# Two-layer graph network on one core: a fourth chunk of the second pass by gathered lists, and dense tiles for the first 128 nodes in five blocks

## The chip, the core and the metric

The kernel runs on one core of one Trainium2 chip. Time is device time in microseconds (us), the median of three runs. A core has TensorE (PE in the profile; PEld are its weight loads), VectorE (DVE), ScalarE (ACT), GpSimd (POOL), and SyncE (SP), which here only issues transfers. ACT and POOL issue transfers as well. All arithmetic on PE is float32 but for the small matmuls that make lists; a float32 matmul appears in the trace as two instructions.

## The reference

There are 3327 nodes with 512 features, and a sparse adjacency matrix `adj` (0.27% of it nonzero, more in the rows and columns of the first nodes, and the whole diagonal).

```python
h = jnp.maximum(_layernorm(x), 0.0)                     # layer 0
x = x + adj @ (relu(adj @ (h @ W1) + b1) @ W2) + b2     # 512 -> 128 -> 512
h = jnp.maximum(_layernorm(x), 0.0)                     # layer 1
attn_a = sigmoid(concat([adj @ h, h]) @ Wa.T + ba)
attn_b = sigmoid(concat([adj @ h, h]) @ Wb.T + bb)
hh = h @ W_sa
e = where(adj != 0, exp(-leaky_relu(s_left[:, None] + s_right[None, :], 0.01)), 0)
x_a = (e / (sum(e) + 1e-5)) @ hh
x_b = adj @ (h @ W_gcnb) + b_gcnb
out = x + sigmoid(attn_a * x_a + attn_b * x_b)
```

`s_left` and `s_right` are two products of `hh` with halves of `a_sa`.

## The kernel before

The rows are padded to 3328, 26 blocks of 128 nodes; the transposed adjacency `adjT` is in HBM. The kernel goes over the graph three times.

**First pass** (the loop around line 660): u = h W1 for all blocks, then for each chunk of columns the sum over all 26 row blocks j, acc_u += u[j]^T adjT[j, chunk], each from a dense load of adjT (512 KB a load, six buffers). The chunks, in the order `back`, are blocks 22-25, 18-21, 14-17, 10-13, 2-5, 6-9 and 0-1. The result, after relu, is g (128 features a node), kept on chip and also stored as `g_dram`.

While a chunk passes, VectorE reduces it to a flag for each node and each group of 32 columns: does the node have an edge into the group (line 670)? In the next chunk's time `make_lists` turns the flags into lists of node numbers, with scans, small matmuls (p_list, line 573) and comparisons. A list of block i has `rooms[i]` places of 64 nodes for each of its four groups; block 0 (the "hub") has none and stays dense. Some of the nodes are left out of the lists because a dense tile takes them: `extra[i]` counts such tiles, one for the block's own diagonal (`OWN`) and one for the first 64 nodes (`TOP`). These tiles are loaded in the first pass by `load_own` (line 210 on) over ACT's queue, two DMAs of 16 KB each. If a list were too short, a flag is raised, and a guarded part at the kernel's end does the work again densely.

With the lists, POOL gathers from HBM with indirect DMAs (line 181), one for each place and half: the column pieces of adjT (128 pieces of 32 numbers, `ae`, by `gather_adj`), rows of g (`g_row`, 128 rows of 512 bytes) and rows of the second layer (`hr`, `rows`: 128 rows of 2080 bytes). Column pieces are gathered one at a time behind chosen matmuls (`gather_behind`) in the first pass, and later where `gather_one` and `fetch_ae` have room.

**Second pass**: adj times g. The last `LISTED = 3` chunks (12 blocks) are done by lists in `list_sums` (matmul at line 911): for each of a block's rooms + extra pairs k, four small matmuls (64 nodes x 32 columns) of the gathered columns with the gathered rows of g, with the block's own g, or with `g_top`, the g of the first 64 nodes. Then ACT copies the sums (line 921), PE turns them (pt_s, line 926), ACT copies again (line 931). The other chunks, 3.5 of 512 columns, are done densely in `dense_sums` (line 957), with adjT loaded again. Then for each block `make_row` adds the layer's result to x (px, line 752; line 756), normalizes, makes the scores, and stores the row to `h_dram`.

What PE does in this pass is written out by hand in `PLAN`, a letter and a count each: d one dense matmul of `dense_sums`, s the sums of one listed block, t the turn of a listed chunk, x a row (`make_row`), l the turning of scores, h one hub matmul (block 0 of the third pass needs all rows: `add_hubs`, line 804, with acc_hub from `a_hub` and from the exponentials e_hub), e the making of such an exponential on DVE and ACT. PE takes the steps in this order. `MADE` gives the order in which dense (d) and listed (l) chunks' rows are made. Each step has a planner's cost (`STEP`, 0.93 for d, x and h, 1.1 for s, 0.6 for t, 0.5 for l). Whenever `SPACE` = 1.4 of them have passed since the last and more than `QUIET` = 20 are left, `gather_one` issues a gather behind the PE's last matmul: the next g row where one of the 24 row buffers is free, else the next column piece. Hub matmuls that the plan leaves over are done after it, in `rest_of_hubs`.

**The passage**: SP then issues the loads of W_gcnb, of the weights for the logits, of `h_top` (the rows of the first 64 nodes), of `w_left`, and of the first blocks' own rows (`h_own`, line 1087). h_top, a scratch `junk` and w_left lie in the space of `a_hub`, which the hub's matmuls and exponentials must have left.

**Third pass**: attention, block by block from 25 down to 1, with block 0 first from the hub's sums. For each pair k of a block, `attend` makes the exponentials and `sums` (line 1171) does four 64x64 matmuls over 512 features for each of two accumulators; `turn` (line 1185), `weigh` (p_b line 1225, p_a line 1233) and `finish` give the output. Blocks are pipelined: PE does p_b and p_a of one block, the turn of the next and the sums of the one after. For each block `fetch_ae(2)` gathers two more column pieces, and a block that still lacks pieces gathers them before its rows. A block's row gathers are held back (`pace`) until the sums of three or four blocks earlier are done.

Block i's number of pairs k is rooms[i] + extra[i]. Before: 4 for blocks 14, 15, 17, 18, 21 and 24; 3 for 16, 19, 20, 22, 23 and 25; 5 for 10 and 11; 4 for 12 and 13; 5 for 7 and 8.

## Time and profile before

| what | us |
|---|---|
| median of three runs | 720.23 |
| lowest, highest | 717.16, 721.58 |
| the profiled execution's own time | 803.64 |
| its span, first to last instruction | 801.8 |
| first pass in the span | 0 to 237.8 |
| plan of the second pass | 237.8 to about 404 |
| passage (rest of the hub, first loads and gathers) | about 404 to 450 |
| third pass | about 450 to 802 |

The profile is of one execution, and it is longer than the runs without a profile. In a row of a timeline stand the start and the length in us, the engine, the line of the kernel, the operation, output<-inputs, and how many instructions were merged; what stands in brackets is how long the engine was idle before it, and what released it ("issue": nothing that the profile names; "remote": a releaser that it can't name). A group's mean is in ns. POOL made 424 gathers: 178 of columns, 68 of g rows, 178 of second-layer rows. Of the column gathers 98 were issued before 237.8 us, 39 after 404.

### The profile page before, as it was taken

The numbers are of one execution on the slowest core, as the hardware profiler recorded it, in microseconds if no ns is written. First come the engines' busy times: TensorE is split into PE (matmuls) and PEld (weight loads), VectorE is DVE, ScalarE is ACT, GpSimd is POOL, SyncE is SP. The second block draws the span as 40 slices with busy tenths as digits, with TensorE's granted clock in tenths as the row PEclk, the third lists the DMA queues.
The fourth block names the chain that finished last, engine by engine and source line by source line (L and its number), as shares of the span: only waits on it lengthen the run. The fifth ranks groups of instructions, "written<-read, shape, count | busy, mean of one in ns | idle before, by whom it ended". The sixth has DMA issues, their size and how long they took to land.

```text
span 801.8 us, 11934 instructions
## 1 busy us (share of the span) xinstructions
PE 727.4 (91%) x3723; PEld 392.0 (49%) x3723; DVE 486.1 (61%) x1532; ACT 204.7 (26%) x494; POOL 456.8 (57%) x487
## 2 busy tenths in 40 slices
PE   8999949988999799797996589899999999999995
PEld 7775424433554344344543255344555445555554
DVE  6878947988963245455573077347567466575642
ACT  6770000000000234444460123022223122131311
POOL 2400556766765667766727646776766766676400
PEclk9999969999979999998998699899999999999998
DMA  8789949988849999983368456756665766877410
GB/s 273 250 299 310 304 135 292 322 276 266 274 127 337 337 320 332 365 263 125 119 223 281 128 157 208 224 160 179 213 190 179 224 197 201 241 229 226 135 52 31
DMA packets 105882, 180.47 MB, mean 225 GB/s; under 512 B 21361, under 2 KB 38161, under 8 KB 105810
## 3 DMA queue, kind: packets, MB, share of 16 engines
q1 hardware_dynamic: 63776, 111.91, 41.3%
q0 software_dynamic: 22112, 54.46, 23.9%
q10 hardware_dynamic: 19922, 13.25, 5.3%
q8 instruction: 31, 0.51, 0.3%
q14 instruction: 41, 0.34, 0.1%
HBM read 157.64 MB, written 22.26 MB: 224 GB/s over the span
## 4 chain that ended last, share of the span: by engine, by line
PE 83%; issue 7%; DVE 3%; DMA 2%; another core or an unknown queue 2%; ACT 1%; ACTq 0%; SPq 0%; DVEq 0%
PE acc_u L660 19%; PE acc L1171 14%; PE p_b L1225 12%; PE p_a L1233 12%; PE acc_g L957 9%; PE acc_hub L804 3%; PE pu L381 3%; PE px L752 3%; PE ptt L1185 3%; DMA a<-in_adjT_dram 1%; PE pt L373 1%; PE p_list L573 1%; PE acc_s L911 1%; PE pl L1103 1%
## 5 line engine op out<-in xcount | busy, mean ns | idle before, releaser
L181 POOL DMA_INDIRECT ae<-in_adjT_dram,row_a x178 | 185.3, 1041 | 137.9 <-DVE jb L584 57.4
L660 PE MATMUL acc_u<-a,rows 128*128 128x512 f32 (+1 forms) x364 | 166.7, 596 | 3.9 <-issue 2.9
L181 POOL DMA_INDIRECT hr<-h_rows,row_h x114 | 120.3, 1055 | 54.0 <-issue 27.4
L670 DVE TENSOR_REDUCE most<-a 128x32 f32<-128x1024 f32 (+1 forms) x104 | 104.2, 1010 | 12.9 <-DMA a<-in_adjT_dram 9.9
L1225 PE MATMUL p_b<-W_g_sb,tyT 128*128 128x257 f32 x416 | 101.8, 395 | 8.9 <-issue 7.1
L1233 PE MATMUL p_a<-W_sa_sb,tyT 128*128 128x512 f32 (+3 forms) x224 | 97.0, 576 | 3.4 <-DVE f L1047 1.9
L660 PEld LDWEIGHTS acc_u<-a,rows 128*128 128x128 f32 x364 | 68.6, 200 | 63.7 <-issue 59.3
L181 POOL DMA_INDIRECT rows<-h_rows,row_h x64 | 67.9, 1061 | 54.6 <-PE acc L1171 22.6
L1225 PEld LDWEIGHTS p_b<-W_g_sb,tyT 128*128 128x128 f32 x416 | 78.3, 194 | 42.2 <-issue 16.0
L181 POOL DMA_INDIRECT g_row<-g_rows,row_h x68 | 70.9, 1042 | 34.5 <-issue 14.9
L957 PE MATMUL acc_g<-a,g 128*128 128x512 f32 (+1 forms) x208 | 86.4, 555 | 1.0 <-DMA a<-in_adjT_dram 0.7
L1200 DVE COPY tyT<-ptt 128x512 f32<-128x512 f32 x51 | 35.1, 688 | 78.1 <-issue 35.7
L1233 PEld LDWEIGHTS p_a<-W_sa_sb,tyT 128*128 128x128 f32 x224 | 42.4, 193 | 43.6 <-issue 39.7
L1171 PE MATMUL acc<-hr,ae 64*64 64x512 f32 x456 | 60.7, 601 | 2.2 <-issue 1.9
L957 PEld LDWEIGHTS acc_g<-a,g 128*128 128x128 f32 x208 | 38.6, 193 | 39.4 <-issue 36.3
L756 DVE SCALAR_TENSOR_TENSOR xb<-px,xb 128x512 f32<-128x512 f32 x26 | 17.9, 688 | 56.2 <-PE px L752 44.8
L390 ACT ACTIVATE gT<-acc_u,b_col 128x512 f32<-128x512 f32 (+1 forms) x7 | 4.6, 657 | 169.6 <-PE acc_u L660 80.5
L1024 DVE SCALAR_TENSOR_TENSOR a_hub<-h_own,w_own 128x512 f32<-128x512 f32 x52 | 35.5, 683 | 9.7 <-DMA h_own<-h_rows 9.6
L1107 ACT COPY s_left<-pl 64x64 f32<-64x64 f32 x42 | 8.7, 207 | 124.4 <-PE pl L1103 66.2
L1171 PEld LDWEIGHTS acc<-hr,ae 64*64 64x64 f32 x456 | 20.1, 136 | 36.5 <-issue 35.1
L279 DVE SCALAR_TENSOR_TENSOR ae<-ae 128x192 f32<-128x192 f32 (+2 forms) x31 | 12.2, 405 | 37.5 <-ACT ae L278 30.3
L1171 PE MATMUL acc<-rows,ae 64*64 64x512 f32 x256 | 32.8, 592 | 1.6 <-issue 1.4
(166 smaller groups left out, 983.6 us busy)
## 6 DMA issues: line engine op xcount, KB each, us to landing
a<-in_adjT_dram SPq DMA_DIRECT2D x129, 512.0 KB
h_rows<-rows SPq DMA_DIRECT2D x26, 260.0 KB
h_own<-h_rows SPq DMA_DIRECT2D x26, 260.0 KB
x<-in_x_dram SPq DMA_DIRECT2D x26, 256.0 KB
xb<-in_x_dram SPq DMA_DIRECT2D x26, 256.0 KB
x<-xb ACTq DMA_DIRECT2D x26, 256.0 KB
x1b<-x SPq DMA_DIRECT2D x26, 256.0 KB
out_dram<-va SPq DMA_DIRECT2D x25, 256.0 KB
```

The costliest lines, as they stand in the source:

```text
L181: return nc.gpsimd.indirect_dma_start(out=dst, out_offset=None, in_=table, in_offset=bass.IndirectOffsetOnAxis(ap=rows, axis=0), bounds_ch ...
L381: nc.tensor.matmul(pu[:, :HID], hT[:, k, :], W1_sb[:, k, :], start=(k == 0), stop=(k == KD - 1))
L660: added = nc.tensor.matmul(acc[:, :w], u[j], a[:, :w], start=(j == 0), stop=(j == NB - 1))
L670: reduced = nc.vector.tensor_reduce(most[:, : w // GW, j : j + both], tiles.rearrange("p k (b i) -> p b k i", i=GW), axis=AX.X, op=ALU.max ...
L752: on_pe[0] = last_row[2] = nc.tensor.matmul(px, sTs.pop(i), W2_sb, start=True, stop=True)
L804: return nc.tensor.matmul(acc_hub[k], s, made_row(i)[:, :D], start=(n == 0), stop=(n == NB - 1))
L957: on_pe[0] = nc.tensor.matmul(acc[:, :w], g[j], a[:, n % per, :], start=(n == 0), stop=(n == NB - 1))
L1024: nc.vector.scalar_tensor_tensor(junk, h[:, :D], 1.0, w_own[:, s, :], op0=ALU.mult, op1=ALU.mult, accum_out=node[i][:, 1 + s : 2 + s],)
L1171: added = nc.tensor.matmul(taken[i]["acc"][h][q * HALF : (q + 1) * HALF, :], both[half_p, q * n + k, :], taken[i][k0][k][half_p, q, :D], s ...
L1200: last = nc.vector.tensor_copy(dst, src)
L1225: last = nc.tensor.matmul(p_b[n][:, :WH], tyT[:, k, 0, :], W_g_sb[:, k, n * WH : (n + 1) * WH], start=(k == 0), stop=(k == KD - 1),)
L1233: last = nc.tensor.matmul(p[:, : c1 - c0], tyT[:, k, 1, :], W_sa_sb[:, k, c0:c1], start=(k == 0), stop=(k == KD - 1),)
```

## The change

- `LISTED` goes from 3 to 4: blocks 10-13 of the second pass are done by lists. 2.5 chunks of 512 columns stay dense. `MADE` and `PLAN` are written anew: 78 + 4 dense matmuls instead of 104 + 4 (the last few calls of either find nothing left), 16 s instead of 12, 4 t instead of 3, 41 h instead of 32, 26 x in both. `SPACE` is 1.3. With both constants the plan issues 104 gathers; now 86 are rows of g and 18 columns, where they were 68 and 36.
- `NEXT`: blocks 7, 8, 20, 22 and 23 take the first 128 nodes' columns (two tiles of 64 nodes) and their own as dense tiles, three extra tiles each. Their rooms go from 4 to 3 (7, 8) and from 3 to 2 (20, 22, 23). Their pairs k go from 5 to 6 and from 3 to 5. The sum of rooms goes from 89 to 84, that of extra tiles from 26 to 39.
- g_top and h_top become two tiles each, with twice the loads.
- The lists are made in batches of at most 14 places (`LIST_W`) instead of 18, and the first block of the first chunk is a batch of its own; `most` has one buffer instead of two.
- In the last chunk of the first pass a column is gathered behind every third matmul instead of every second, and the four column gathers behind the first dense matmuls of the second pass are gone.

```diff
-LISTED = 3
+LISTED = 4
+LIST_W = 14
-MADE = "dldldld"
+MADE = "dldlldl"
 PLAN = """
-d26 s1 d2 x1 d1 x1 d3 s1 x1 l1 d3 x1 e2 s1 d8 s1 d3 t1 d3 x1 s1 x1 e2 d7 x1 s1 d3 x1 e2 d4 s1
-d1 x1 d3 l1 x1 e2 s1 d3 t1 x1 h2 s1 d1 x1 e1 h2 d2 x1 h1 s1 h1 x1 e2 h2 d4 x1 s1 h2 x1 e2 h2
-d3 s1 d1 x1 h1 t1 h1 x1 e2 h2 d7 x1 h2 d2 x1 e2 h2 d8 x1 h2 d2 x1 e2 h2 d4 x1 h2 x1 h2 x1 h2
-x1 h2
+d19 s1 d5 s1 d4 x1 s1 x1 d4 x1 l1 d1 s1 d1 x1 e2 t1 d6 x1 s1 d3 x1 e2 d3 s1 d2 x1 h2 s1 d1 x1
+e2 h2 d1 s1 d2 t1 d2 x1 h1 l1 x1 e2 s1 h3 d3 x1 h2 d2 x1 e2 s1 h2 d6 x1 h1 s1 h1 x1 e2 h2 d7 x1
+s1 h2 t1 x1 e2 h2 d4 s1 x1 h2 d2 x1 e2 h3 s1 h2 x1 h2 x1 e2 h2 s1 h2 x2 e2 s1 h2 t1 h2 x2 h3 x1
+h1 x1
 """
-SPACE, QUIET = 1.4, 20.0
+SPACE, QUIET = 1.3, 20.0
-TOP = 3, 4, 5, 9, 10, 11, 21, 24
-
-OWN = TOP + (1, 6, 7, 8, 12, 13, 14, 15, 17, 18)
+NEXT = 7, 8, 20, 22, 23
+
+TOP = NEXT + (3, 4, 5, 9, 10, 11, 21, 24)
+
+OWN = TOP + (1, 6, 12, 13, 14, 15, 17, 18)
...
-    rooms = [0, 8, 7, 5, 4, 4, 4, 4, 4] + n_blocks * [3]
-    rooms[21] = rooms[24] = 2
+    rooms = [0, 8, 7, 5, 4, 4, 4, 3, 3] + n_blocks * [3]
+    for i in 20, 21, 22, 23, 24:
+        rooms[i] = 2
...
-    extra = [int(i in OWN) + int(i in TOP) for i in range(NB)]
+    extra = [int(i in OWN) + int(i in TOP) + int(i in NEXT) for i in range(NB)]
...
-                rows = slice(0, HALF) if k else cols
+                rows = slice((k - 1) * HALF, k * HALF) if k else cols
...
-                            nc.vector.memset(flag[:HALF, groups, 0:1], 0.0)
+                            covered = (extra[c0 // P + b] - 1) * HALF
+                            nc.vector.memset(flag[:covered, groups, 0:1], 0.0)
...
-                    if not batches or sum(rooms[k] for k, _ in batches[-1]) + rooms[i] > CW // NT:
+                    full = batches and sum(rooms[k] for k, _ in batches[-1]) + rooms[i] > LIST_W
+                    if not batches or full or (nth == 0 and len(batches) == 1 and q == 0):
...
-            most = l0p.tile([P, MG, NB], F32, tag="most", name=f"most_{c0}")
+            most = l0p.tile([P, MG, NB], F32, tag="most", name=f"most_{c0}", bufs=1)
...
-                if j % 4 if w == CW else j % 2:
+                if j % 4 if w == CW else j % 3 == 1:
                     gather_behind(added)
...
-                                        t = g_top if kk else g[i]
+                                        t = g_tops[kk - 1] if kk else g[i]
...
-        g_top = ae[1][:, : HID // GW, GW:]
+        g_tops = [ae[1][:, k * HID // GW : (k + 1) * HID // GW, GW:] for k in range(2)]
...
-                    if c == 0 and n < 4:
-                        gather_behind(on_pe[0])
...
-        h_top, junk, w_left = (free_hub[:, k * ROW : k * ROW + w] for k, w in enumerate((ROW, D, D)))
-        for h in range(2):
-            nc.sync.dma_start(h_top[h * HALF : (h + 1) * HALF, :], h_dram[:HALF, :])
+        *h_tops, junk, w_left = (
+            free_hub[:, k * ROW : k * ROW + w] for k, w in enumerate((ROW, ROW, D, D))
+        )
+        for k, t in enumerate(h_tops):
+            for h in range(2):
+                nc.sync.dma_start(
+                    t[h * HALF : (h + 1) * HALF, :], h_dram[k * HALF : (k + 1) * HALF, :]
+                )
```

More of the change, by code (lines that the diff above doesn't have):

```diff
@@ L556, in make_lists @@
                 f0 = first[batch[0][0]] + batch[0][1] * rooms[batch[0][0]]
-                at = l0p.tile([P, CW // NT, 2, HALF], BF16, tag="at", name=f"at_{f0}")
+                at = l0p.tile([P, LIST_W, 2, HALF], BF16, tag="at", name=f"at_{f0}")
                 for i, q in batch:
@@ L577, in make_lists @@
                 yield
-                past = l0p.tile([P, CW // NT, NB], BF16, tag="past", name=f"past_{f0}", bufs=1)
+                past = l0p.tile([P, LIST_W, NB], BF16, tag="past", name=f"past_{f0}", bufs=1)
                 nc.vector.tensor_tensor(
@@ L582, in make_lists @@
                 )
-                jb = l0p.tile([P, CW // NT], F32, tag="jb", name=f"jb_{f0}")
+                jb = l0p.tile([P, LIST_W], F32, tag="jb", name=f"jb_{f0}")
                 nc.vector.tensor_reduce(jb[:, :m], past[:, :m, :], axis=AX.X, op=ALU.add)
@@ L935 @@
         hubs = add_hubs()
-        g_top = ae[1][:, : HID // GW, GW:]
+        g_tops = [ae[1][:, k * HID // GW : (k + 1) * HID // GW, GW:] for k in range(2)]
         def load_g_top():
-            for h in range(2):
-                nc.scalar.dma_start(
-                    g_top[h * HALF : (h + 1) * HALF],
-                    g_dram[:HALF, :].rearrange("j (k f) -> j k f", f=GW),
-                )
+            for k, t in enumerate(g_tops):
+                for h in range(2):
+                    nc.scalar.dma_start(
+                        t[h * HALF : (h + 1) * HALF],
+                        g_dram[k * HALF : (k + 1) * HALF, :].rearrange("j (k f) -> j k f", f=GW),
+                    )
         order = [i for c0, w in back for i in range(c0 // P, (c0 + w) // P)]
@@ L1126, in attend @@
                 if k0 + k < extra[i]:
-                    h = h_top if k else h_own[i]
+                    h = h_tops[k0 + k - 1] if k0 + k else h_own[i]
                     hr.append(h.unsqueeze(1).to_broadcast([P, 2, ROW]))
@@ L1265 @@
         free_hub = a_hub.rearrange("p j i -> p (j i)")
-        h_top, junk, w_left = (free_hub[:, k * ROW : k * ROW + w] for k, w in enumerate((ROW, D, D)))
-        for h in range(2):
-            nc.sync.dma_start(h_top[h * HALF : (h + 1) * HALF, :], h_dram[:HALF, :])
+        *h_tops, junk, w_left = (
+            free_hub[:, k * ROW : k * ROW + w] for k, w in enumerate((ROW, ROW, D, D))
+        )
+        for k, t in enumerate(h_tops):
+            for h in range(2):
+                nc.sync.dma_start(
+                    t[h * HALF : (h + 1) * HALF, :], h_dram[k * HALF : (k + 1) * HALF, :]
+                )
         nc.sync.dma_start(w_left, w_dram[0, :].partition_broadcast(P))
```

## Prediction

> **What bounds the kernel now.** I read the page's busy rows and chain first, then busy time by stage, then TensorE's (PE's) timeline inside the second pass and the third.
>
> ```profile
> PE 727.4 (91%) x3723; PEld 392.0 (49%) x3723; DVE 486.1 (61%) x1532; ACT 204.7 (26%) x494; POOL 456.8 (57%) x487
> ...
> PE 83%; issue 7%; DVE 3%; DMA 2%; another core or an unknown queue 2%; ACT 1%; ACTq 0%; SPq 0%; DVEq 0%
> ```
>
> PE is on the chain for 83% of the 801.8 us span, some 666 us. "issue" and "unknown queue" are 9% more, 73 us: stretches in which PE, ScalarE (ACT) and VectorE (DVE) stand together and no work is named. The profiled execution took 803.64 us, the median of the runs shown is 720.23. The 83 us between them are about those stretches, so I take it (an inference) that the plain runs hardly have them. My sum is made of full-clock durations of PE work: +x on 803.64 is +x on 720.23.
>
> The busy time by stage (columns: PE, PEld, DVE, ACT, POOL, then granted clock, DMA share, GB/s) for first pass, plan of the second pass, passage to the third, third pass:
>
> ```profile
> 0.00:237.80 237.80, 214.74 (x1067) 121.48 (x1067) 187.66 (x479) 50.96 (x113) 113.85 (x161) 0.94 0.82 263
> 237.80:410.00 172.20, 157.05 (x739) 74.83 (x734) 84.37 (x294) 63.32 (x161) 113.96 (x109) 0.96 0.80 267
> 410.00:452.00 42.00, 26.41 (x94) 13.43 (x96) 14.77 (x55) 7.83 (x21) 25.80 (x25) 0.80 0.71 227
> 452.00:802.00 350.00, 329.25 (x1838) 182.23 (x1831) 199.25 (x705) 82.55 (x202) 203.23 (x193) 0.98 0.59 178
> ```
>
> PE fills three stages; the passage (410 to 452) it fills to 63% only. So work taken from PE's plan is worth its duration, work taken from the passage need not be. Inside the second pass:
>
> ```profile
> 246.63 15.72 PE L957 MATMUL acc_g<-a,g 128*128 128x512 f32 x36
> ...
> 298.83 0.66 PE L926 MATMUL pt_s<-ident,s 128*128 128x128 f32 x4 [0.89 <-issue]
> ...
> 335.07 0.66 PE L926 MATMUL pt_s<-ident,s 128*128 128x128 f32 x4 [4.06 <-issue]
> ...
> 339.94 0.42 PE L911 MATMUL acc_s<-g,ae 64*32 64x128 f32 x8
> 340.18 0.83 PE L911 MATMUL acc_s<-g_row,ae 64*32 64x128 f32 x24
> 340.94 1.13 PE L957 MATMUL acc_g<-a,g 128*128 128x512 f32 x2
> ```
>
> Dense matmuls run back to back, 0.437 us an instruction and two to a matmul. A block's list sums of 32 instructions last from 339.94 to 340.94: 1.0 us, 0.25 us for each tile pair k. A turn (pt_s) waits for ACT's copy of the sums.
>
> **The second pass, step by step.**
> - *A dense chunk goes.* 26 matmuls x 2 x 0.437 = **-22.7 us**. Its loads go too: 26 x 256 KB = 6.8 MB, against 18 more gathered rows of g (64 KB each, 1.2 MB). PE waited for such a load for 0.67 us in the pass's timeline, so the relief is worth 0 to 0.7 (7.6, if I believed the chain's one DMA piece at 255 us, under which PE was busy). I take 0.
> - *List sums come.* Blocks 10 to 13 have 5, 5, 4 and 4 pairs k, blocks 20, 22 and 23 two more each: 24 x 0.25 = 6.0, four pt_s 0.5: **+6.5**.
> - *Hub matmuls move into the plan.* The plan has 41 h steps instead of 32. Each is two instructions of 0.43: 9 x 0.86 = **+7.7** in the plan. What comes off the passage? There PE ends the hub and stands:
>
> ```profile
> 421.93 2.74 PE L804 MATMUL acc_hub<-rows,e_hub 128*128 128x512 f32 x6
> 429.20 6.61 PE L1225 MATMUL p_b<-W_g_sb,tyT 128*128 128x257 f32 x16 [4.54 <-issue]
> ```
>
> and VectorE over the same time:
>
> ```profile
> 427.11 0.69 DVE L1024 SCALAR_TENSOR_TENSOR a_hub<-h_own,w_own 128x512 f32<-128x512 f32 x1 [9.61 <-DMA h_own<-h_rows]
> ```
>
> DVE stood 9.61 us for h_own, and its copy of tyT for that p_b came behind. The first row gathers start at 416.51, after the last row was stored. This chain of last row, store, loads, gathers has no hub matmul in it; the hub matmuls only fill PE meanwhile, and PE already has 4.5 us to spare. Nine fewer there are worth 0. Bounds: 0, or -7.7 if PE sets the passage.
> - *Turns.* The first turn had three d (2.7 us) between sums and transpose and still waited 0.89, so the handoff is about 3.6. In the 4.06 us wait ACT and DVE stood too, on a releaser that the profile calls remote; I leave it out as one of the standing stretches, and with it the third turn's 5.75. The new order leaves two steps (1.7 us) ahead of each of four turns: 4 x 1.9 = 7.6, against 3 x 0.9 = 2.7 now: **+4.9**. Behind a waiting pt_s stand all of PE's plan and, at the last turn, the last four rows. Bounds: 0 (ACT's copy itself is 0.59) and +16 (four waits of some 4.7 against those 2.7). Here the Trainium skill speaks against the change: its page "TensorE: Matmul & The Clock Gate", Part 1, has the clock halve after an idle window of about 3.4 us. The trace agrees: after the 5.75 us wait two hub instructions took 1.91 us instead of 1.02. By the row of 0.89 my turns wait 1.9 us and the clock stays; if they waited 4 to 6 us, the rule adds about 3 us at each, up to 12 in all, and the sum of this change would be near +27 instead of +4.
> - *POOL.* Both plans gather 104 times; the new one makes 86 of them rows of g. In its solid stretches POOL takes 1.30 us from gather to gather (1.00 and 0.30 of issue), on the mean duration of 1042 ns 1.34. The new plan's last needed row is gather 94. POOL: 5 us from the pass's start, 94 x 1.34 = 126, some 2.5 for landing: about 133 us. PE's work up to the sums of block 13: 56.3 for d, 18.9 for x, 28.4 for h, 16.3 for s, 5 for t, l and lists: 125; with three turn waits (5.7) and the 3.2 it waits at the l step now, 134. So the gathers just make it: **0**; with prompt turns it would wait for POOL instead, so these two costs don't add.
>
> Plan: -22.7 + 6.5 + 7.7 + 4.9 = -3.6.
>
> **The third pass.** Here PE goes from one block to the next without naming a wait for a gather:
>
> ```profile
> 526.00 1.95 PE L1171 MATMUL acc<-rows,ae 64*64 64x512 f32 x16
> 527.76 1.04 PE L1171 MATMUL acc<-hr,ae 64*64 64x512 f32 x8
> 528.73 3.73 PE L1225 MATMUL p_b<-W_g_sb,tyT 128*128 128x257 f32 x16
> ```
>
> Three pairs k in 2.73 us; five pairs elsewhere (673.13 to 677.58) 4.45: 0.86 a pair. Blocks 20, 22, 23 go from 3 to 5 pairs, blocks 7 and 8 from 5 to 6: 8 x 0.86 = **+6.9**. Ten row gathers and ten column gathers go, but of the 168 column gathers left some 18 are now put off from the second pass to here: POOL +8 x 1.3 = 10 us, with 203 of 350 us busy: hidden; without cover, the eight columns that block 1 would have to fetch late are 10 us.
>
> **The rest.** Twenty fewer p_list instructions: -0.6. Thirteen own and first-nodes tiles more, 26 loads of 16 KB on ACT's queue in the first pass. What pieces of 128 bytes cost there, from the first pass's DMA queues (packets, MB, share of 16 engines):
>
> ```profile
> q1 hardware_dynamic: 30516, 54.38, 68.5%
> ...
> q0 software_dynamic: 3104, 1.40, 2.8%
> ```
>
> The column gathers (q0) have such pieces: 1.40 MB in 2.8% of 237 us, 211 GB/s, where the big loads (q1) make 335. The skill's page "DMA: Bandwidth & Descriptors", Specifications, asks for 512 bytes or more for line rate, and its rules call transfers under 64 KB mostly overhead. By the row 0.43 MB are 2.0 us; by the rule, if each of the 26 held the engines for the 0.95 us that the page gives for 64 KB, 25 (an estimate from that page). I take the row. PE names 1.0 us of waits for adjacency loads in that pass, so most is hidden: **+1.0** (0 to 2.0). Narrower lists and single `most` buffers: VectorE runs them in order, 0. Two h_top and two g_top loads more; the second h_top and w_left now lie over hub tiles that are used last, and h_own is queued behind them on SP: **+0.5** (0 to 1.5).
>
> Sum: -3.6 + 6.9 - 0.6 + 1.0 + 0.5 = **+4.2**: 807.8 profiled, **724.4** on the median. I say 724, own range 718 to 731.
>
> **Rivals.**
> 1. *PE's work alone counts* (710): the passage is PE's and gives the 7.7 back, the turns are prompt: -22.7 + 6.5 + 6.9 - 0.6 = -9.9. For it: 83% of the chain. Against: 4.54 us idle behind the hub. Chance 0.28.
> 2. *POOL becomes the bound of the second pass* (slower, 733): place: sums of blocks 12 and 13; price: 94 times what a gather takes over 1.34, and all that follows waits, px of the last rows too. It decides from 1.36 us. For it: the pace asks for a gather each 1.3 units of about 0.92 us, 1.20 us; single gathers took 1.4 + 0.3. At 1.44 it is +9. Against: gathers of 1.00 are the most. Chance 0.18.
> 3. *The turns wait as the longest ones did, with the halved clock* (740 or more). Chance 0.08.
> 4. *It doesn't do its work*: a list that overflows starts the dense repetition at the end, hundreds of us. Counted on the reference's inputs, the fullest lists are 192 of 192 (block 7) and 128 of 128 (block 23), none over. Chance near 0.
>
> **How the numbers follow.** About 1% is what a measurement of this kernel can tell from no change: 713 to 727.4. The forecast holds 0.46: 0.37 inside, 0.09 above. Rival 1: 0.23 below, 0.05 inside. Rivals 2 and 3: 0.26 above. So 0.23 faster, 0.42 same, 0.35 slower. The range for 8 in 10 reaches from rival 1 (710, less 2 for the loads) to beyond rival 2: 708 to 738.
>
> **What would show it.** Right: acc_g 26 matmuls fewer; the last row stored 2 to 6 us earlier from the pass's start; PE idle ahead of p_b of block 0 grown from 4.5 to about 12 us; blocks 20, 22, 23 each 1.7 us longer. Wrong: s sums that wait for g_row (rival 2); p_b of block 0 following the hub at once (rival 1); turns that wait under 1 us, or over 4.

## The result, and the profile after

The changed kernel takes 738.75 us (median of four runs, 736.93 to 740.9) where the kernel before takes 720.34: a ratio of 1.0264, 95% interval 1.022 to 1.0307, so 18.4 us slower. The prediction was 724, 4 us slower, with a range of 708 to 738; the measured time lies just above it. A second measurement of the unchanged pair, `after_again`, gave 1.028 (1.0239 to 1.032).

One thing is needed to read the numbers: on some occasions the kernel before itself took 718 to 720 us, as in the recorded times, and on others 798 to 808, so each run below is compared only with the kernel before beside it, and the latter are marked "beside 798".

The recorded profile of before was of the second kind. `before_clean`, the same kernel profiled on the first kind, has a span of 716.7 us and is what the changed kernel's profile stands beside from here on. The changed kernel's busy rows and its chain:

```profile
PE 694.6 (94%) x3911; PEld 383.6 (52%) x3911; DVE 488.1 (66%) x1563; ACT 203.7 (28%) x497; POOL 456.0 (62%) x479
...
PE 46%; DMA 1%; DVE 1%; ACT 1%; issue 0%; POOL 0%; ACTq 0%; DVEq 0%
```

The chain goes back only to 368 us this time, the end of the plan, so it says nothing of the first two stages. The stages do. Busy time by stage, the columns as before (length; PE, PEld, DVE, ACT, POOL; granted clock, DMA share, GB/s), for first pass, plan, passage (last px to the first p_a) and third pass. First `before_clean`:

```profile
0.00:213.70 213.70, 207.39 (x1067) 118.82 (x1067) 184.84 (x476) 50.92 (x113) 110.10 (x160) 0.99 0.90 291
213.70:361.80 148.10, 144.28 (x728) 70.12 (x723) 83.29 (x288) 61.20 (x155) 113.00 (x107) 1.00 0.90 308
361.80:397.30 35.50, 31.34 (x135) 15.05 (x134) 17.75 (x68) 10.87 (x28) 24.57 (x25) 1.00 0.80 265
397.30:716.70 319.40, 309.64 (x1805) 177.38 (x1803) 199.11 (x705) 80.82 (x201) 210.31 (x198) 0.99 0.67 198
```

and the changed kernel:

```profile
0.00:220.30 220.30, 209.37 (x1041) 119.38 (x1041) 184.00 (x483) 50.93 (x112) 109.51 (x151) 0.98 0.90 284
220.30:373.50 153.20, 142.03 (x894) 71.58 (x894) 83.65 (x296) 60.04 (x155) 109.63 (x105) 0.97 0.80 259
373.50:414.50 41.00, 26.94 (x113) 12.44 (x112) 17.49 (x64) 11.15 (x28) 23.54 (x24) 0.79 0.75 249
414.50:739.10 324.60, 316.26 (x1869) 180.21 (x1867) 202.95 (x723) 81.59 (x203) 213.31 (x200) 1.00 0.63 186
```

Every stage grew: by 6.6, 5.1, 5.5 and 5.2 us, 22.4 in all. PE's busy time grew by 2 us only (692.65 to 694.6), its idle time by 20.4. And the 2 us hide more: by the prediction's own terms (-22.7 + 6.5 + 6.9 - 0.6) PE should have become 9.9 us less busy. The difference is the clock column: the trace's record of the granted clock has it at half for 37.5 us, in seven stretches, ahead of the kernel's tail (a window over one of them, 395.1 to 405.3, shows 0.50), where `before_clean` has 3.4. PE is at work in some 27 of these 37.5 us. At half the clock its instructions take twice as long (3.69 us instead of 1.95 below), so about 13.5 us of its busy time are the clock's (an estimate from these figures; 1.7 in `before_clean`). -9.9 and +11.8 are the 2 us. So the loss is waits, and slow matmuls behind the waits.

In the plan PE waits at two places that matter, a turn and the last sums (PE's timeline of the changed kernel):

```profile
296.65 1.11 PE L932 MATMUL pt_s<-ident,s 128*128 128x128 f32 x4 [3.85 <-ACT s L927]
...
359.99 0.64 PE L917 MATMUL acc_s<-g_row,ae 64*32 64x128 f32 x4 [4.58 <-DMA g_row<-g_rows,row_h]
361.22 0.64 PE L917 MATMUL acc_s<-g_row,ae 64*32 64x128 f32 x4 [0.59 <-DMA g_row<-g_rows,row_h]
361.79 2.07 PE L810 MATMUL acc_hub<-rows,a_hub 128*128 128x512 f32 x2
```

The second wait, 5.2 us, is for rows of g that have not landed yet: the sums of block 13. The hub's two instructions behind it take 2.07 us instead of 1.02: the halved clock. In the passage:

```profile
388.15 3.63 PE L1230 MATMUL p_b<-W_g_sb,tyT 128*128 128x257 f32 x16
401.65 3.69 PE L1176 MATMUL acc<-rows,ae 64*64 64x512 f32 x16 [9.43 <-DVE ae L283]
...
408.24 1.56 PE L1176 MATMUL acc<-h_own,ae 64*64 64x512 f32 x8 [1.99 <-DVE ae L283]
```

where `before_clean` has

```profile
383.20 3.74 PE L1225 MATMUL p_b<-W_g_sb,tyT 128*128 128x257 f32 x16 [1.51 <-DVE tyT L1200]
387.31 1.95 PE L1171 MATMUL acc<-rows,ae 64*64 64x512 f32 x16
...
392.77 1.09 PE L1171 MATMUL acc<-h_own,ae 64*64 64x512 f32 x8 [2.65 <-DVE ae L279]
```

p_b of block 0 now follows the hub at once, and the idle time stands behind it, 9.43 us for the exponentials of block 25. The 16 instructions after that wait take 3.69 us instead of 1.95. In the first pass the changed kernel falls behind in two places. Its turn pg of the third chunk comes at 120.51 where `before_clean` has 116.56, and that of the fifth at 176.42 where it has 168.50; elsewhere the difference hardly changes or shrinks. The changed kernel's timeline at the third chunk's end ("ACTq" is ACT issuing transfers, here eight loads of half a small tile each):

```profile
111.09 8.63 ACTq L343 DMA_DIRECT2D ae<-in_adjT_dram  x8
...
114.45 1.98 PE L666 MATMUL acc_u<-a,rows 128*128 128x512 f32 x4 [1.79 <-DMA a<-in_adjT_dram]
...
119.77 0.69 ACT L394 ACTIVATE gT<-acc_u,b_col 128x512 f32<-128x512 f32 x1 [29.81 <-DMA ae<-in_adjT_dram]
120.51 0.66 PE L403 MATMUL pg<-ident,gT 128*128 128x128 f32 x4 [1.24 <-ACT gT L394]
```

ACT is 8.63 us at issuing eight 16 KB loads; its relu gT for the chunk's end comes after them, and PE's turn pg waits 1.24 us for it. Meanwhile the big adjacency loads come late (1.79 us here, 3.3 in three waits from 110 to 118 us). In `before_clean` gT is 2 us ahead of its pg:

```profile
114.55 0.69 ACT L390 ACTIVATE gT<-acc_u,b_col 128x512 f32<-128x512 f32 x1 [24.25 <-PE acc_u L660]
116.56 0.60 PE L399 MATMUL pg<-ident,gT 128*128 128x128 f32 x4
```

It names no wait of pg at all, and 0.6 us for adjacency. The second place is a step of the list-making in the fifth chunk, which waits for VectorE; first the changed kernel, then `before_clean`:

```profile
155.68 1.88 PE L579 MATMUL p_list<-step,at 128*64 128x27 bf16 x24 [2.02 <-DVE at L568]
157.48 8.12 PE L666 MATMUL acc_u<-a,rows 128*128 128x512 f32 x12
```

```profile
151.56 2.69 PE L573 MATMUL p_list<-step,at 128*64 128x27 bf16 x36 [0.41 <-DVE at L562]
```

Behind the wait the clock is halved: twelve instructions of acc_u take 8.12 us, where at 129.72 twelve take 5.42. The packets, MB and share of 16 engines of ACT's queue in the first pass, in the changed kernel and in `before_clean`:

```profile
q10 hardware_dynamic: 19106, 6.66, 12.3%
```

```profile
q10 hardware_dynamic: 15362, 6.24, 10.9%
```

The share is 27.1 us of 220.3, and 23.3 of 213.7. So the loads take 3.8 us of the engines, not the 2.0 that I took, and a little over half of the 6.6 that the stage lost.

The third pass is as steady as before. Block 23, with five pairs k instead of three, from 426.00 to the next p_b at 430.54:

```profile
426.12 1.05 PE L1176 MATMUL acc<-h_own,ae 64*64 64x512 f32 x6
426.91 1.98 PE L1176 MATMUL acc<-a_hub,ae 64*64 64x512 f32 x16
428.63 1.98 PE L1176 MATMUL acc<-hr,ae 64*64 64x512 f32 x16
430.54 1.79 PE L1230 MATMUL p_b<-W_g_sb,tyT 128*128 128x257 f32 x7
```

4.54 us; in `before_clean` it took 2.8 (408.85 to 411.66). a_hub in the second line is the name under which the two tiles of the first 128 nodes stand.

### The profile page after: what moved, and what is told of

The parts are those of the page before. It is cut to its first block, busy times and chain, and to the rows that moved or that the text cites. A ratio compares the mean times of both kernels' runs of the same rounds, so it can differ in the third digit from the quotient of the medians.

```text
span 739.1 us, 12339 instructions
## 1 busy us (share of the span) xinstructions
PE 694.6 (94%) x3911; PEld 383.6 (52%) x3911; DVE 488.1 (66%) x1563; ACT 203.7 (28%) x497; POOL 456.0 (62%) x479
## 5 line engine op out<-in xcount | busy, mean ns | idle before, releaser
L185 POOL DMA_INDIRECT ae<-in_adjT_dram,row_a x168 | 175.8, 1046 | 117.4 <-PE acc_u L666 75.0
L666 PE MATMUL acc_u<-a,rows 128*128 128x512 f32 (+1 forms) x364 | 161.1, 581 | 3.3 <-DMA a<-in_adjT_dram 3.3
L185 POOL DMA_INDIRECT hr<-h_rows,row_h x104 | 110.3, 1060 | 35.9 <-issue 22.2
L185 POOL DMA_INDIRECT g_row<-g_rows,row_h x86 | 89.1, 1036 | 37.2 <-PE acc_g L964 15.6
L1230 PE MATMUL p_b<-W_g_sb,tyT 128*128 128x257 f32 x416 | 97.0, 385 | 0.5 <-ACT tyT L1203 0.5
L964 PE MATMUL acc_g<-a,g 128*128 128x512 f32 (+1 forms) x156 | 62.1, 536 | 2.0 <-DMA a<-in_adjT_dram 2.0
L1238 PEld LDWEIGHTS p_a<-W_sa_sb,tyT 128*128 128x128 f32 x224 | 41.7, 189 | 37.5 <-issue 35.9
L1176 PE MATMUL acc<-hr,ae 64*64 64x512 f32 x416 | 49.0, 595 | 0.0
L964 PEld LDWEIGHTS acc_g<-a,g 128*128 128x128 f32 x156 | 28.8, 194 | 26.4 <-issue 21.8
L1029 DVE SCALAR_TENSOR_TENSOR a_hub<-h_own,w_own 128x512 f32<-128x512 f32 x52 | 35.5, 682 | 0.1
L1176 PEld LDWEIGHTS acc<-hr,ae 64*64 64x64 f32 x416 | 16.8, 137 | 28.8 <-issue 26.6
L1190 PEld LDWEIGHTS ptt<-ident,ty 128*128 128x128 f32 x208 | 24.3, 141 | 14.3 <-issue 13.2
```

The costliest lines, as they stand in the source:

```text
L185: return nc.gpsimd.indirect_dma_start(out=dst, out_offset=None, in_=table, in_offset=bass.IndirectOffsetOnAxis(ap=rows, axis=0), bounds_ch ...
L666: added = nc.tensor.matmul(acc[:, :w], u[j], a[:, :w], start=(j == 0), stop=(j == NB - 1))
L964: on_pe[0] = nc.tensor.matmul(acc[:, :w], g[j], a[:, n % per, :], start=(n == 0), stop=(n == NB - 1))
L1029: nc.vector.scalar_tensor_tensor(junk, h[:, :D], 1.0, w_own[:, s, :], op0=ALU.mult, op1=ALU.mult, accum_out=node[i][:, 1 + s : 2 + s],)
L1176: added = nc.tensor.matmul(taken[i]["acc"][h][q * HALF : (q + 1) * HALF, :], both[half_p, q * n + k, :], taken[i][k0][k][half_p, q, :D], s ...
L1190: moved = nc.tensor.transpose(pt[:, k * P : (k + 1) * P], ty[h][:, k * P : (k + 1) * P], ident)
```

## The experiments

### The kernel before again, and each half of the change alone (beside 798)

`before_again` is the kernel before without an edit.

> The kernel before, unchanged, for a second profile. If the stretches in which all engines stood together belong to the first profile alone, the span is about 720 us, and the first pass takes 210 to 215, the plan of the second 150 to 155, the passage 35 to 40, the third pass 315 to 320. If they belong to the kernel, the span is about 800 again.

Measured: 796.49 us, near the 803.64 of the recorded profile. What lay between 720 and 803 belonged to the occasion, not to profiling.

`next_only` is the changed kernel with the old second pass:

```diff
-LISTED = 4
+LISTED = 3
...
-SPACE, QUIET = 1.3, 20.0
+SPACE, QUIET = 1.4, 20.0
...
-                if j % 4 if w == CW else j % 3 == 1:
+                if j % 4 if w == CW else j % 2:
...
+                    if c == 0 and n < 4:
+                        gather_behind(on_pe[0])
```

What is left out are `MADE` and `PLAN`, which are those of before.

> Only the dense tiles for the first 128 nodes in five blocks (with the smaller rooms and the list batches of the change); three listed chunks, the old plan, pace and order. Theory A (my sum): third pass +6.9, list sums of blocks 20, 22 and 23 +1.5, first pass +1: about 730 us against 720. Theory B (the 26 loads of small pieces hold up the first pass): first pass +5 to +10 as well: 735 to 740. Theory C (the loss is made by the fourth listed chunk and its order, through gathered rows): within 4 us of before.

`listed_only` is the changed kernel without the dense tiles:

```diff
-NEXT = 7, 8, 20, 22, 23
+NEXT = ()
...
-OWN = TOP + (1, 6, 12, 13, 14, 15, 17, 18)
+OWN = TOP + (1, 6, 7, 8, 12, 13, 14, 15, 17, 18)
...
-    rooms = [0, 8, 7, 5, 4, 4, 4, 3, 3] + n_blocks * [3]
-    for i in 20, 21, 22, 23, 24:
-        rooms[i] = 2
+    rooms = [0, 8, 7, 5, 4, 4, 4, 4, 4] + n_blocks * [3]
+    rooms[21] = rooms[24] = 2
```

> Only the fourth listed chunk with the new plan, pace and order; rooms and extra tiles as before, so 92 rows of g instead of 86 and 178 columns. Theory A: -22.7 for the chunk, +5.1 for its list sums and turn, +7.7 for the hub matmuls moved, +5 for turns: about 715 us. Theory C (gathers bound the second pass): six more rows of g at 1.3 us each make it slower than the whole change's plan there, 5 us and more of waits for g_row: 725 to 735. Theory B: no more first-pass time than before.

Measured: `next_only` 1.0009 of the kernel before (0.9978 to 1.004), `listed_only` 1.0454 (1.0374 to 1.0534). `next_only` looks as if the tiles cost nothing, where my terms for them (third pass 6.9, loads 1.0, six more list pairs 1.5, less 0.6) come to 8.8 us. But both kernels keep the narrower lists of the change, and these alone make the kernel before faster on such occasions, to 0.9868 and 0.9923 of its time (`narrow_lists` and `narrow_lists_2` below). Set against that, the tiles cost 0.9 to 1.4%, 7 to 11 us (an estimate across occasions), about what I had said. The fourth listed chunk alone costs 37.8 on the medians, more than either theory expected. The two are not a sum: the whole change took 1.0346 on such an occasion (`after_again_2` below), the listed chunk alone 1.0454. POOL's busy time in the third pass and the stage's length were 176.7 us and 341.0 in `next_only`, 199.0 and 340.9 in `before_again`, 209.5 and 360.9 in `after_again_2`, 229.8 and 377.4 in `listed_only`. From 199 us on the two grow together. That is a correlation of stages; which of the two sets the other these runs do not show. It pointed at POOL.

### The unchanged pair, rows of g first, and the hub moved back

`before_clean` and `after_again` are unedited.

> The kernel before, unchanged, for a profile to set beside that of the changed kernel. Theory A (my sum: the plan of the second pass is PE's work, so the loss lies in the turns' waits and the third pass) expects its plan, from the first dense matmul to the last row's px, to be about as long as the changed kernel's 152.7 us plus 4, and its third pass 7 us shorter. Theory C (POOL's gathers have become the bound of the new plan) expects before's POOL to have gaps in the plan, PE without a wait for a g row, and the plan not longer than the changed one's.

> The changed kernel, unchanged, as the base for the runs beside it. If the loss is the kernel's own, the ratio is that measured already (1.026, within 1.022 to 1.031); if another chip makes another mix of waits, it may lie from 1.01 to 1.05.

Measured: 718.52 us for the one run of `before_clean`; 740.62 for `after_again`, 1.028 (1.0239 to 1.032). Before's plan is 148.1 us and the changed one 153.2, so A's "4 us longer before" is wrong by its sign; its third pass is 5.2 us shorter, A's part that holds. PE has no wait for a g row in before's plan, as C expected; but POOL has no gaps there either, which C did not. It gathers columns that nobody waits for yet: row 68, the last of g, starts 103 us after the pass's first matmul.

`rows_first`:

```diff
                 n = g_count["taken"]
-                if n < len(g_slots) and n // NU * NU < g_count["summed"] // NU * NU + GR:
-                    made = gather_g()
-                else:
+                if n >= len(g_slots):
                     made = next(columns, None)
+                elif n // NU * NU < g_count["summed"] // NU * NU + GR:
+                    made = gather_g()
+                else:
+                    owed[0] += SPACE
+                    made = None
```

> The changed kernel, but POOL gathers all 86 rows of g ahead of the columns that stand between them; the columns follow. Theory C (POOL's 94 gathers from 12.5 us after the pass's start set the sums of block 13): up to eight gathers fewer ahead of row 86 are 8 x 1.3 = 10 us, so the wait of 5.2 us for a g row goes, the last row comes about 5 us earlier, and the kernel is 4 to 6 us faster than the changed kernel. Theory A (PE's work sets the plan, POOL just makes it): no difference, within 1 us.

Measured: 733.1 us, 1.0179 (1.0132 to 1.0225), 7.5 less than `after_again`. Its stages:

```profile
0.00:220.40 220.40, 208.12 (x1042) 119.39 (x1042) 184.15 (x483) 50.88 (x112) 109.08 (x151) 0.98 0.90 284
220.40:365.60 145.20, 139.95 (x894) 70.91 (x894) 83.52 (x296) 60.06 (x155) 104.49 (x100) 0.99 0.84 273
365.60:406.80 41.20, 27.99 (x113) 12.44 (x112) 17.53 (x64) 11.15 (x28) 27.42 (x28) 0.79 0.77 248
406.80:731.60 324.80, 316.26 (x1869) 180.19 (x1867) 203.26 (x723) 81.53 (x203) 215.02 (x202) 0.99 0.63 186
```

Only the plan moved, by 8.0 us (153.2 to 145.2; it is 155.3 in the profile of `after_again`), and PE no longer waits for a g row. Three of POOL's gathers in the changed kernel, the first row of g, the last column ahead of the last two rows, and the last row:

```profile
232.82 1.00 POOL L185 DMA_INDIRECT g_row<-g_rows,row_h  x1 [11.30 <-PE acc_g L964]
...
355.87 1.00 POOL L185 DMA_INDIRECT ae<-in_adjT_dram,row_a  x1 [0.30 <-issue]
...
358.48 1.00 POOL L185 DMA_INDIRECT g_row<-g_rows,row_h  x1 [0.31 <-DMA ae<-in_adjT_dram,row_a]
```

Counted from the pass's first matmul, in the changed kernel the first g row is gathered after 12.5 us, row 86 is gather 94 and starts at 138.2 (a pitch of 1.351); in `rows_first` row 86 is gather 86 and starts at 126.0. The last sums come at 141.1 and 134.6 us. So the gathers set the end of the changed plan: shown, and the gain is more than the 4 to 6 expected since the halved clock behind the wait went as well (plan's clock 0.97 to 0.99).

`hub_back` leaves nine hub matmuls to the passage; a letter o that does nothing and counts 0.93 keeps the pace of the gathers:

```diff
-d19 s1 d5 s1 d4 x1 s1 x1 d4 x1 l1 d1 s1 d1 x1 e2 t1 d6 x1 s1 d3 x1 e2 d3 s1 d2 x1 h2 s1 d1 x1
-e2 h2 d1 s1 d2 t1 d2 x1 h1 l1 x1 e2 s1 h3 d3 x1 h2 d2 x1 e2 s1 h2 d6 x1 h1 s1 h1 x1 e2 h2 d7 x1
-s1 h2 t1 x1 e2 h2 d4 s1 x1 h2 d2 x1 e2 h3 s1 h2 x1 h2 x1 e2 h2 s1 h2 x2 e2 s1 h2 t1 h2 x2 h3 x1
-h1 x1
+d19 s1 d5 s1 d4 x1 s1 x1 d4 x1 l1 d1 s1 d1 x1 e2 t1 d6 x1 s1 d3 x1 e2 d3 s1 d2 x1 o2 s1 d1 x1 e2
+o2 d1 s1 d2 t1 d2 x1 o1 l1 x1 e2 s1 o3 d3 x1 h2 d2 x1 e2 s1 h2 d6 x1 h1 s1 h1 x1 e2 h2 d7 x1 s1
+h2 t1 x1 e2 h2 d4 s1 x1 h2 d2 x1 e2 h3 s1 h2 x1 h2 x1 e2 h2 s1 h2 x2 e2 s1 h2 t1 h2 x2 h3 x1 o1
+x1
...
-            "e": make_e_hub,
+            "e": make_e_hub, "o": lambda: None,
```

> The changed kernel with 32 hub matmuls in the plan instead of 41: nine are left to the passage, as many as there were before; the pace of the gathers is kept. Theory A (PE's work sets the plan and the passage has room): the plan is 9 x 0.86 = 7.7 us shorter and the passage no longer, so 6 to 8 us faster than the changed kernel. Theory C (POOL sets the sums of block 13, whatever PE does ahead of them): what PE saves it waits at those sums, the nine come back in the passage, within 2 us of the changed kernel or slower by up to 5.

Measured: 738.12, 1.0252 (1.0219 to 1.0286), 2.5 less than `after_again`. Plan and passage:

```profile
217.80:371.40 153.60, 138.27 (x876) 69.44 (x876) 81.70 (x289) 59.31 (x153) 110.17 (x105) 0.94 0.79 259
371.40:413.20 41.80, 33.65 (x131) 15.27 (x130) 19.12 (x71) 11.66 (x31) 23.93 (x23) 0.88 0.74 240
```

The plan loses 18 PE instructions and is not shorter; the passage gains 18 and is 0.8 longer. The small gain sits in the first pass (217.8), where nothing was edited: that stage, the same code in all of them, took 217.8 to 221.2 us in four profiled executions. A's 6 to 8 is ruled out.

### Tile loads, lists, h_top, and the clock (beside 798, then once beside 719)

Four kernels ask about the first pass and the passage. `no_tiles` is the changed kernel with an edit in load_own:

```diff
         for k in range(extra[i]):
+            if i in NEXT and k >= int(i < 9):
+                continue
```

> The changed kernel without the 26 loads of its 13 added dense tiles; the tiles stay zero, so those edges are left out of the sums, and everything else runs as before. Theory T (the tile loads make the first pass longer: they jam ACT's queue and the adjacency loads behind them come late): the first pass is back from 220.3 us to 214 to 215, and the kernel 5 to 7 us faster than the changed one. Theory L (the narrower lists and the single buffer of the flags do it): first pass still 219 to 221, no gain. My prediction put the loads at 1.0 (0 to 2.0), the lists at 0.

`narrow_lists` is the kernel before with

```diff
+LIST_W = 14
...
-                    if not batches or sum(rooms[k] for k, _ in batches[-1]) + rooms[i] > CW // NT:
+                    full = batches and sum(rooms[k] for k, _ in batches[-1]) + rooms[i] > LIST_W
+                    if not batches or full or (nth == 0 and len(batches) == 1 and q == 0):
...
-            most = l0p.tile([P, MG, NB], F32, tag="most", name=f"most_{c0}")
+            most = l0p.tile([P, MG, NB], F32, tag="most", name=f"most_{c0}", bufs=1)
```

> The kernel before with the changed kernel's lists alone: batches of at most 14 places, the first block a batch of its own, one buffer for the flags. Theory L: the first pass grows from 213.7 us to 217 to 220 and the kernel is 3 to 6 us slower than before. Theory T: within 1.5 us of before.

`one_htop` is `rows_first` with

```diff
-        for k, t in enumerate(h_tops):
+        for k, t in enumerate(h_tops[:1]):
```

> The kernel with the rows of g first (rows_first), without the two loads of the second h_top tile, which keeps old numbers, so the attention of five blocks is not the reference's. Theory H (the added h_top load holds up the row gathers of block 25): from the last px to the sums of block 25 it is 25.5 us as before the change, not 27.5, and the kernel is 2 us faster than rows_first. Rival (the gathers land late for another reason): 27 to 28 us, no difference.

`warm_passage` is `rows_first` with this in first_sums, behind the turn of block 0 (p_a's bank is handed in by `weigh`):

```diff
+            for _ in range(9):
+                with queued(added):
+                    added = nc.tensor.matmul(p_a, ident, W_sa_sb[:, 0, :], start=True, stop=True)
```

> The kernel with the rows of g first (rows_first), with nine matmuls of 512 columns added that serve nothing, in PE's 8.65 us wait for block 25's exponentials; the results are untouched. Theory G (PE's idle in the passage halves its granted clock, and the matmuls after it pay): no halved clock behind the wait, the stretch from the sums of block 25 to p_a of block 0 is 10.0 us as before the change instead of 13.6, and the kernel is 3 to 4 us faster than rows_first. Rival (those sums are slow since their rows come late): no difference or up to 1 us slower.

All four fell beside 798. `no_tiles` 1.0359 (1.0303 to 1.0415), `narrow_lists` 0.9868 (0.981 to 0.9925), `one_htop` 1.0411 (1.0334 to 1.0489), `warm_passage` 1.032 (1.0216 to 1.0423). `no_tiles` does not show the shorter first pass of theory T (228.8 us, against 229.7 in `after_again_2`). From the last px to the sums of block 25 `one_htop` took 27.7 us and `warm_passage` 27.8: no support for theory H. But beside 798 the kernel before itself takes 29.3 there (`before_again`), so the 25.5 that H expects could not be seen, and H stays untested. In `warm_passage` the first 16 instructions of block 25 took 1.95 us, in `one_htop` 3.67: theory G's local sign. Its time was lost again in the next wait for DVE (10.47 us against 8.49). They were run again with a base beside them:

> The changed kernel, unchanged, as the base for the runs beside it, on whatever chip they fall: 1.024 to 1.032 of the kernel before where that takes 720 us, 1.03 to 1.045 where it takes 798.

> The kernel of no_tiles again, beside the changed kernel itself (its 26 added tile loads left out, those edges missing from the sums). Theory T (the loads make the first pass longer): first pass 5 to 7 us shorter than the changed kernel's, and the whole 5 to 7 us. Theory L (the narrower lists): no shorter.

> The kernel of narrow_lists again (the kernel before with the changed kernel's lists). Theory L: first pass 3 to 6 us longer than before's 213.7 and the kernel 3 to 6 us slower than before. Theory T: within 1.5 us of before; where before takes 798 us it was 1.3% faster, which neither theory expects.

> The kernel of warm_passage again (rows of g first, nine idle matmuls in the wait of the passage). Theory G (the halved clock after PE's idle): the first 16 matmul instructions of block 25 take 1.95 us instead of 3.69, the stretch from them to p_a of block 0 10.0 us instead of 13.6, the kernel 3 to 4 us faster than rows_first's 1.018 of before. Rival: no difference.

Again beside 798: `after_again_2` 1.0346 (1.0215 to 1.0477), `no_tiles_2` 1.0371 (1.024 to 1.0502), `narrow_lists_2` 0.9923 (0.9885 to 0.996), `warm_passage_2` 1.0381 (1.0231 to 1.053). No gain from either edit of the changed kernel there (first pass 230.8 us in `no_tiles_2`): on these occasions T's 5 to 7 us are missing, and for the 720 case it is inconclusive. The narrower lists make the kernel before faster there (first pass 227.3 instead of 237.0), which speaks against L; why, is open. Once more:

> The kernel of no_tiles once more (the changed kernel without its 26 added tile loads, those edges missing from the sums), since the two before fell among runs in which the kernel before takes 798 us. If before takes 720 us here: theory T expects the first pass to last 214 to 215 us instead of 220 to 221, no wait of a turn for ACT's g, and 1.018 to 1.021 of before instead of 1.028; theory L 219 to 221 us and 1.026 to 1.03.

> Three edits in one kernel, each in a stage of its own: rows of g first, the nine idle matmuls in the passage, and the 26 added tile loads left out (those edges are missing from the sums). Where the kernel before takes 720 us: theory T (tile loads) expects a first pass of 214 to 215 us, theory L (narrower lists) 219 to 221; theory G (halved clock after PE's idle) expects 1.95 us for the first 16 matmul instructions of block 25 and 10.0 us from them to p_a of block 0, its rival 3.69 and 13.6; the plan stays at rows_first's 145 us. T and G together: 1.018 of before less 9 us, 1.004 to 1.008; L and the rival: 1.017 to 1.02. Where before takes 798 us I expect no difference from rows_first's kind, 1.03 to 1.04, and the stages tell nothing on T.

> The kernel of joined again, with the same expectations: where the kernel before takes 720 us, theory T a first pass of 214 to 215 us against 219 to 221 for theory L; theory G 1.95 us for the first 16 matmul instructions of block 25 and 10.0 us from them to p_a of block 0 against 3.69 and 13.6; T and G together 1.004 to 1.008 of before, L and the rival 1.017 to 1.02. Where before takes 798 us: no difference from 1.03 to 1.04.

`joined` puts the edits of `rows_first`, `no_tiles` and `warm_passage` together, each in a stage of its own. `no_tiles_3` 1.0339 (1.0234 to 1.0445) and `joined` 1.029 (1.0163 to 1.0417) fell beside 798 and 808, and told nothing new. `joined_2` fell beside a kernel before of 718.64 us: 722.69 us, 1.0062 (1.0038 to 1.0087), what T and G together expected. Its stages, of one execution:

```profile
0.00:212.90 212.90, 207.78 (x1042) 119.61 (x1042) 183.44 (x483) 50.79 (x112) 110.78 (x151) 0.98 0.90 291
212.90:357.90 145.00, 139.93 (x893) 70.63 (x893) 83.31 (x296) 60.02 (x155) 104.06 (x100) 0.99 0.84 274
357.90:397.50 39.60, 32.84 (x130) 14.97 (x129) 17.40 (x64) 11.05 (x28) 27.23 (x27) 0.91 0.78 248
397.50:722.10 324.60, 316.35 (x1869) 180.30 (x1867) 203.25 (x723) 81.61 (x203) 217.16 (x204) 1.00 0.63 187
```

and its passage on PE:

```profile
376.66 7.89 PE L1301 MATMUL p_a<-W_sa_sb,ident 128*128 128x512 f32 x18
386.80 2.56 PE L1181 MATMUL acc<-rows,ae 64*64 64x512 f32 x16 [2.25 <-DVE ae L285]
...
397.55 3.60 PE L1243 MATMUL p_a<-W_sa_sb,tyT 128*128 128x512 f32 x8
```

The first pass is 212.9 us against `rows_first`'s 220.4: 7.5 us for 26 loads of 16 KB (with the 217.8 to 221.2 of that stage, 4.9 to 8.3). PE names no wait for adjacency or for gT there any more, and none at the list step of the fifth chunk. It keeps the narrower lists and is still 0.8 us shorter than before's, so theory L is out. In the passage, from the sums of block 25 to p_a it is 10.75 us against 13.6, the clock 0.91 against 0.79: theory G holds, in this one execution. A wait of 2.25 us remained, since the rows landed 1.4 us later in this run than in `rows_first`, and with it 3.4 us of halved clock; so of the 2.85 us only 1.6 is seen in the stage.

No version here beats the kernel before. `joined_2` comes nearest, and it lacks loads that it would have to make somewhere.

## Why the prediction was wrong, step by step

| stage | before | changed | predicted difference | measured | rows_first | joined_2 |
|---|---|---|---|---|---|---|
| first pass | 213.7 | 220.3 | +0.4 | +6.6 | 220.4 | 212.9 |
| plan | 148.1 | 153.2 | -3.6 | +5.1 | 145.2 | 145.0 |
| passage | 35.5 | 41.0 | +0.5 | +5.5 | 41.2 | 39.6 |
| third pass | 319.4 | 324.6 | +6.9 | +5.2 | 324.8 | 324.6 |
| span | 716.7 | 739.1 | +4.2 | +22.4 | 731.6 | 722.1 |

Three terms failed: POOL's gathers, the tile loads and the passage stood in the sum with 0, 1.0 and 0.5 us and cost 8.0, 7.5 and 5.5. What is left, 1.4 us, is near the 2.7 of all the other terms. So the sign of the forecast came out right by luck: what made the kernel slower was hardly in it.

- **Dense chunk, -22.7: right.** acc_g has 52 instructions fewer and PE 22.5 us less of them (84.6 to 62.1).
- **List sums, +6.5: right by the rate.** Five pairs from 341.62 to 342.85 us are 1.23, 0.25 a pair.
- **Hub, +7.7 in the plan and 0 back: half right.** `hub_back` shows nothing to be had in either place: the passage gave nothing back, as said, but neither did the plan cost it, since POOL set the plan's end. With POOL out of the way (`rows_first`) the plan is 2.9 us shorter than before's, and there the sum of -3.6, with the 7.7 in it, comes out within 1 us. In part that is luck: ahead of the last px stand eleven more hub matmuls than before and not nine (82 instructions against 60, two of before's come after it), 1.7 us, and PE's shorter waits for loads give them back (1.0 us against 2.4).
- **Turns, +4.9: the sum near, the picture wrong.** I had four waits of 1.9 us. One turn waited 3.85, three not (clean before: 1.1 in all instead of my 2.7). With the 3.4 us of halved clock about that turn, at most 1.7 us of work, it is 2.7 to 4.4.
- **POOL, 0: the first failed step, 8.0 us.** "POOL: 5 us from the pass's start, 94 x 1.34" gave 133 against PE's 134. The count, the pitch (1.351) and PE's 134 (134.6 in `rows_first`, where PE waits for no row) were right; the start was not, and I had named no row for it. A row of g is gathered after the last chunk's g is stored (the store is issued at 225.22): 12.5 us after the start, and the recorded profile of before had it in plain sight, 11.4 us after 237.8:

```profile
249.25 1.00 POOL L181 DMA_INDIRECT g_row<-g_rows,row_h  x1 [4.53 <-DMA a<-in_adjT_dram]
```

   With 12 instead of 5, 94 gathers end at 138 plus landing, and rival 2 is the forecast. It was rival 2's place and mechanism, though by a late start and not by a slower gather; its sign, sums that wait for g_row, is what the profile shows. POOL stands idle for 11.30 us ahead of that first row (3.09 in `before_clean`), since the change took away the column gathers that filled the place; eight columns at the pitch of 1.35 would have fitted there. That was not tried.
- **Third pass, +6.9: right in PE's work** (busy 309.64 to 316.26, +6.6), of which 1.4 was taken out of its idle time.
- **Tile loads, +1.0: the second failed step, 7.5 us** (`joined_2`). I set row against rule, 2.0 by the packets' share of the engines against an estimate of 25 from the Trainium skill's page "DMA: Bandwidth & Descriptors" (26 times the 0.95 us that its section Bandwidth gives for 64 KB), and took the row. Neither is right. On the engines they are 3.8; the timeline shows the rest in front of them: ACT held for 8.63 us at eight loads, its relu behind them, big loads late, and PE's waits followed by the halved clock. That the cost goes through ACT's queue is read from the timeline and not tried by itself; that the loads are the cause is shown, on the one occasion beside 719.
- **Passage, +0.5: the third failed step, 5.5 us.** The view was of the disturbed profile, where p_b of block 0 waited 4.54 us on nothing named; in `before_clean` it waits 1.51 and the stage is 88% PE (31.34 of 35.5). Then 2.8 us are PE's halved clock behind a wait of 9.43: 10.0 us from the sums to p_a before, 12.8 after, 10.75 with idle matmuls in the wait. The other 2.7 us are ahead of it: from the last px to those sums 25.5 us before, 28.2 after, because the rows of block 25 land later. Of these, 1.0 is that POOL starts on them later, 10.5 us after the last px instead of 9.5, behind the store of the last row, which SP issues at 7.2 instead of 6.1; the rest lies between the gathers and their landing. DVE's timeline of the changed kernel, its waits for them:

```profile
394.04 0.23 DVE L1147 TENSOR_TENSOR ae<-s_left,rows 128x64 f32<-128x64 f32 x1 [7.34 <-DMA rows<-h_rows,row_h]
397.52 0.23 DVE L1147 TENSOR_TENSOR ae<-s_left,rows 128x64 f32<-128x64 f32 x1 [3.26 <-DMA rows<-h_rows,row_h]
399.49 0.23 DVE L1147 TENSOR_TENSOR ae<-s_left,hr 128x64 f32<-128x64 f32 x1 [1.74 <-DMA hr<-h_rows,row_h]
```

  The second h_top load would have been my guess, and `one_htop`, beside 798, cannot tell. Why they land later stays open.
- **The clock.** I let the turns be the only place where the Trainium skill's rule ("TensorE: Matmul & The Clock Gate", Part 1: half clock after an idle window of some 3.4 us) could bite. The halved stretches, of 3.4 us or multiples of it as that page has the window, came at two waits of the first pass, the turn, the g rows, the hub and twice in the passage, not at the turns alone, and the two of the first pass at waits shorter than that window (2.02 and 2.27 us). The recorded profile showed such a place outside the turns: p_b behind its wait of 4.54 us took 6.61 us for 16 instructions, 3.73 in the third pass; both rows stand in the prediction.
- **The excess of the recorded profile.** That the 83 us of "issue" are hardly in the plain runs held (716.7 clean), but I then read bounds of stages, the passage above all, off that profile.

The signs: acc_g as said, block 23 +1.7 as said. The last row came 5 us later and not 2 to 6 earlier; the idle ahead of p_b did not grow but moved behind it. p_b following the hub at once, rival 1's sign, did not mean rival 1: a sign at one instruction is worth little if the wait can move to the next.

## What to carry to other kernels

When work is turned from matmuls into gathers, make the gather engine's own timetable: when its first needed index or row exists, how many gathers stand ahead of the last needed one, and the pitch; and let nothing that is needed later stand in that queue (here eight columns ahead of row 86 were 8 us). Price small loads not by their bytes alone: look at what stands behind them on the issuing engine's queue. A PE wait of 2 us or more can cost its length and 1.7 to 5 us of slow matmuls about it (half of the 3.4 to 10.2 us stretches seen here, an estimate for a PE that is busy all through them), so slack that is given up in several places is paid for in each.

## What the runs showed of the hardware

- The granted clock halved already around waits of 2.02 and 2.27 us (the p_list steps at 155.68 and 184.68 in the changed kernel: halved for 6.8 us from 156.1 and 3.4 us from 186.9), while after a wait of 2.65 us in `before_clean` (392.77) and one of 3.01 us in `rows_first` (119.71) it stayed full. The length of one wait alone does not tell.
- Nine matmuls that serve nothing, put into a wait, kept the clock of those after it: 1.95 us for 16 instructions in `warm_passage`, 3.67 to 3.69 without them.
- Where the kernel before takes 798 us, PE starts some instructions in step with POOL's gathers, with no releaser named; in PE's timeline of `before_again`:

```profile
325.10 0.27 PE L911 MATMUL acc_s<-g_row,ae 64*32 64x128 f32 x1 [0.39 <-issue]
326.51 0.27 PE L911 MATMUL acc_s<-g_row,ae 64*32 64x128 f32 x1 [1.14 <-issue]
327.95 0.27 PE L911 MATMUL acc_s<-g_row,ae 64*32 64x128 f32 x1 [1.17 <-issue]
```

  One instruction each 1.4 us, while POOL issues a g row each 1.3. What makes such an occasion is open.
